# Layer 1's mixer in a 32-graph network: B and C as one product, step sizes beside the gate's product, slice norms spread by one product, two graphs' heads in turn

## The chip, the cores and the metric

One core of a Trainium2 chip runs the whole network in one launch. Times are device microseconds. The time that counts is the median of the runs; a profiled execution shows where it goes. TensorE is called PE below, its weight loads PEld, VectorE DVE, ScalarE ACT, GpSimd POOL and SyncE SP, as the profile has them.

## The reference, cut to what matters

32 graphs of 512 nodes with 256 features pass two layers, each a graph network and a feed-forward part, each on a normed input and added to it. What changes is in the feed-forward part of layer 1, a mixer: every node is softly assigned to 64 slices in each of 8 heads, the slices are averaged into tokens, the 64 tokens of a graph pass a state-space scan in both directions, and the result is handed back to the nodes.

```python
def _L1_ffn_ref(x, ...):
    ...            # sw = softmax over 64 slices, per node and head
    ...            # st = sw-weighted sum of fx / (sum of sw over nodes + 1e-5)
    ot = _hydra(st, ...)
    out = jnp.einsum('bhgc,bhng->bhnc', ot, sw).transpose(0, 2, 1, 3).reshape(B, N, D_INNER)
    return out @ out_w.T + out_b

def _hydra(u, in_w, conv_w, conv_b, dt_bias, A_log, Dp, fcD_w, norm_w, out_w):
    zxbcdt = u @ in_w.T                       # 512 z, 512 x, 64 B, 64 C, 16 dt
    z = zxbcdt[..., :D_INNER]
    xBC = zxbcdt[..., D_INNER:D_INNER + CONV_DIM]
    dt = zxbcdt[..., -2 * H:]
    dt = jnp.concatenate([dt[..., :H], jnp.flip(dt[..., H:], axis=1)], axis=0)
    dt = jax.nn.softplus(dt + dt_bias)
    ...                                       # causal convolution of 3 taps over xBC, then silu
    ...                                       # scan: h = h * exp(-dt * exp(A_log)) + dt * B x; y = C h
    y = y + x_og * jnp.repeat(x_og @ fcD_w.T + Dp, P, axis=-1)
    yg = y * jax.nn.silu(z)
    yg = yg * jax.lax.rsqrt(jnp.mean(jnp.square(yg), -1, keepdims=True) + 1e-05) * norm_w
    return yg @ out_w.T
```

Here D_INNER is 512 (8 heads of 64), and there are 64 tokens for each graph.

## The kernel before

Layer 0 (`layer0_sorted`) fills the first half of the span, with the setup of layer 1 threaded through its end. Layer 1 is `layer1_plain`, a set of Python generators whose steps are laid one after the other at build time; nothing branches on the chip.

Two streams are woven. `attentions()` goes through the 32 graphs one by one: `prepare(b)` loads and norms a graph and makes its masks and projections, `attention(b)` makes the weights (`att`, L1215), the products `avp` (L1248) and `adp` (L1255), and `norm(b)` closes the graph. `mixer(g)` goes through 16 groups of two graphs (GB = 2). The loop at the end of `layer1_plain` draws from `mixer`, and at each of its yields advances `attentions` by the number yielded times PACE. A yield of 7 in `scan` thus stands for some six steps of attention that are written into the queues at this place. After that each engine works off its own queue in order; the order within a queue is nearly that of the code, though the framework's scheduler lets an instruction pass another where it expects it to be ready first.

A group goes through these stages, with the tile names that the profile shows:

- `slices(b, j, yT, rn)`, once for each of the two graphs: norm, logits `lgp`, the softmax `sw` on DVE (L1338 to L1343), the slice sums `yTp`, the transposed weights `swT` whose copy on ACT also accumulates the slice norms, and `rn`, their reciprocal (L1355, L1356). `rn` has one column for each graph and chunk of 128 (two heads by 64 slices) on 128 partitions.
- `tokens`: the products `uTp` (L1367), then `rnp` (L1373), which brings the reciprocals from the partitions to the columns and repeats them over 64 partitions: 16 products of a broadcast column with half of the identity. ACT copies it to `scale`, DVE makes the tokens `uT` (L1380, L1382).
- `scan`, head: `xp` (L1401), the x part of the input projection, transposed; `bcp` (L1410), B and C as two products of 64 rows each; `dtp` (L1429), the step sizes twice in the order of the directions on halves of the partitions, and once more with tokens on partitions (L1394 through `tok_matmul`); `zp` (also L1394), the gate, 512 columns. They are copied or read by `xpad` and `bpad` (ACT), `sp` (DVE L1436, then the softplus) and `z` (ACT Silu, L1451). The convolutions are on DVE (`conv`, L1418 and L1420), their Silu on ACT (L1456, L1463). `la` (L1468) and `seg` (L1482) follow from the step sizes.
- `scan`, middle, after a yield of 7: `gp` (L1488), the products of B and C; `segp` (L1492), from `seg`; `decay` (ACT L1494), `xtp`, `qp`, and `mix` (DVE, to L1511).
- `scan`, after another yield of 7: `yp` (L1518), sixteen products of 64x64 on 64 columns, first the eight heads of graph 0 on partitions 0 to 63, then those of graph 1 on 64 to 127; `y` (DVE L1521 to L1523), the transposes `yTp` (L1528), `oTp` (L1536), `msp` (L1544), which moves the mean squares `ms` to the partitions of the tokens by products with the identity; `rms` (DVE L1547, POOL L1548); then `vp` (L1558) and `v` (ACT L1560).
- `unslice`, for each graph: `outp` (L1568), the sum, and the store.

All PSUM tiles of these stages and of `prepare` come from one tag, "any", with four banks; attention has four of its own ("pv"). The 512-column tiles `scale`, `xT`, `seg`, `decay`, `xk`, `mix`, `back`, `y`, `yT`, `oT` share one tag, "inner", with six buffers. `inT` holds the transposed input projection in the order of the reference: 512 columns of z, 512 of x, 64 of B, 64 of C, 16 of step sizes (DT0 is where those begin, DIN the end). In the profile one fp32 product counts as two passes, each a weight load and a matmul.

Of the kernel before, what the change touches and what calls it, by code (L numbers as in the profile page):

```python
# [8 lines left out]
F32 = mybir.dt.float32  # L9
# [4 lines left out]
AF = mybir.ActivationFunctionType  # L14
# [5 lines left out]
P = 128  # L20
# [846 lines left out]
def layer1_plain(tc, ident, eps, x2s, ranks, adj, w, out, over, ps):  # L867
# [35 lines left out]
    with ExitStack() as ctx:  # L903
# [51 lines left out]
        bc_w = const("bc_w", [S, 2, KW], w["hy_conv_w"][DI:].rearrange("(c p) k -> p c k", p=S))  # L955
        bc_b = const("bc_b", [S, 2], w["hy_conv_b"][DI:].rearrange("(c p) -> p c", p=S))
        skip = const("skip", [P, H], w["hy_D"].partition_broadcast(P))
        dtb = ctile("dtb", [P, 4, H])
        for i in range(4):
            nc.sync.dma_start(dtb[:, i, :], w["hy_dt_bias"].partition_broadcast(P))  # L960
# [18 lines left out]
        for j in range(GB):  # L979
            tri(side[j * G : (j + 1) * G, 0, :], False)  # L980
            tri(side[j * G : (j + 1) * G, 1, :], True)

# [9 lines left out]
        with tc.tile_pool(name="raw", bufs=2, side="right") as raw:  # L992
# [16 lines left out]
            yield from load_T(inT, w["hy_in_w"], "in")  # L1009
# [349 lines left out]
        def tokens(g, yT, rn, uT):  # L1359

            pu, pn = psum("any", f"uTp{g}"), psum("any", f"rnp{g}")
            uv, nv = (p.rearrange("p (k j g) -> p k j g", k=KC, j=GB) for p in (pu, pn))
# [6 lines left out]
            for k in range(KC):  # L1369
                for i in range(P // C):  # L1370
                    half = slice(i * C, (i + 1) * C)
                    for j in range(GB):
                        nc.tensor.matmul(nv[half, k, j, :], rn[:, j, k : k + 1].to_broadcast([P, C]), ident[:, half],  # L1373
                                         start=True, stop=True)
# [9 lines left out]
        def scan(g, uT):  # L1384
# [14 lines left out]
            for k in range(KC):  # L1399
                for c in range(KC):  # L1400
                    nc.tensor.matmul(px[:, k * T : (k + 1) * T], inT[:, c, DI + k * P : DI + (k + 1) * P],  # L1401
                                     uT[:, c, :], start=c == 0, stop=c == KC - 1)
# [3 lines left out]
            pb = psum("any", f"bcp{g}")  # L1406
            for i in range(2):
                c0 = 2 * DI + i * S
                for c in range(KC):
                    nc.tensor.matmul(pb[:S, i * T : (i + 1) * T], inT[:, c, c0 : c0 + S], uT[:, c, :],  # L1410
                                     start=c == 0, stop=c == KC - 1)
# [13 lines left out]
            pd = psum("any", f"dtp{g}")  # L1425
            for j in range(GB):
                for i in range(2):
                    for c in range(KC):
                        nc.tensor.matmul(pd[i * G : (i + 1) * G, j * H : (j + 1) * H],  # L1429
                                         uT[:, c, j * G : (j + 1) * G],  # L1430
                                         inT[:, c, DT0 + i * H : DT0 + (i + 1) * H],
                                         start=c == 0, stop=c == KC - 1)
# [24 lines left out]
            bcT = sb.tile([S, 2, GB, G], F32, tag="bcT", name=f"bcT{g}", bufs=1)  # L1457
# [783 lines left out]
```

## Time and profile before

| | |
|---|---|
| median of 3 runs | 4578.43 us (4575.21 to 4583.15) |
| the profiled execution | 4587.94 us |
| its span, first to last instruction | 4586.1 us |
| mean granted TensorE clock | 0.943 |
| busy: PE, PEld | 4011.0 (87%), 2462.2 (54%) |
| busy: DVE, ACT, POOL | 3391.6 (74%), 2296.8 (50%), 1743.1 (38%) |

Some groups of the profile that belong to the changed code. x counts passes or instructions over the whole run:

| line, tile | shape | count | busy us, mean ns |
|---|---|---|---|
| L1373 rnp, PE | 128x64 weights, 64 columns | 512 | 20.6, 228 |
| L1410 bcp, PE | 128x64 weights, 128 columns | 256 | 31.4, 276 |
| L1429 dtp, PE | 128x64 weights, 8 columns | 512 | 21.8, 204 |
| L1394 dtp, PE | 128x128 weights, 16 columns | 128 | 17.0, 265 |
| L1394 zp, PE | 128x128 weights, 512 columns | 128 | 58.9, 603 |
| L1518 yp, PE | 64x64 weights, 64 columns | 512 | 34.5, 238 |
| L1544 msp, PE | 128x64 weights, 1 column | 128 | 6.4, 202 |
| L1418, L1420 bcT, DVE | 64x128 | 32, 64 | 8.2, 271 and 19.2, 334 |
| L1451 z, ACT | 128x512 | 16 | 9.6, 597 |

Matmuls are pipelined: the printed mean of one pass is its latency, and passes of one row of a timeline overlap. What a row costs PE is read from its start to the start of the next row. A wait is put down to the work that came last before it.

### The profile page before, as it was taken

Reading aid. Unit: us, or ns where it says so; the run is one execution under the profiler, and the core shown is the slowest. Engines: PE = TensorE matmul, PEld = TensorE weight load, DVE = VectorE, ACT = ScalarE, POOL = GpSimd, SP = SyncE. Lnnn points to the kernel's source line nnn. Section 1 sums busy time; section 2 is a strip of 40 time slices with the busy share of each in tenths; the row PEclk is TensorE's granted clock in tenths of the full one; section 3 lists DMA queues with packets and bytes.
Section 4 is the critical chain, followed back from the end, with each engine's and each line's share of the span. In section 5 each row is a group of like instructions: output and inputs, shape, how many; then the busy total and the mean of one; then the engine's idle time right before and its main releaser. Section 6 shows DMA issues by size and latency. Waiting matters only on the chain.

```text
span 4586.1 us, 56206 instructions
## 1 busy us (share of the span) xinstructions
PE 4011.0 (87%) x19287; PEld 2462.2 (54%) x19287; DVE 3391.6 (74%) x7008; ACT 2296.8 (50%) x4756; POOL 1743.1 (38%) x2036
## 2 busy tenths in 40 slices
PE   5567988889988899878997999999999999999987
PEld 4444655556556566445554355555555555555555
DVE  6668888887788877777775777777777777777763
ACT  2344565556655555555664444544544444554432
POOL 2356544654535644353423233222232333322210
PEclk8778999999999999989998999999999999999998
DMA  4447533654436543464422111111111111111100
GB/s 135 155 141 224 179 125 118 203 185 141 142 116 197 182 148 119 121 225 158 140 89 69 35 54 47 56 53 41 47 47 51 54 56 54 53 49 56 40 15 15
DMA packets 235100, 474.09 MB, mean 103 GB/s; under 512 B 38299, under 2 KB 114075, under 8 KB 234804
## 3 DMA queue, kind: packets, MB, share of 16 engines
q0 software_dynamic: 80256, 282.38, 19.2%
q1 hardware_dynamic: 154548, 188.02, 13.2%
q8 instruction: 154, 2.52, 0.2%
q14 instruction: 142, 1.16, 0.1%
HBM read 413.16 MB, written 57.16 MB: 103 GB/s over the span
## 4 chain that ended last, share of the span: by engine, by line
PE 28%; DVE 25%; DMA 7%; POOL 7%; issue 7%; ACT 4%; DVEq 0%; POOLq 0%; SPq 0%; ACTq 0%
DVE att L1215 4%; PE avp L1248 3%; PE clsp L625 3%; PE gatep L625 3%; DVE acc L639 2%; DMA rows<-table,xs 2%; DVE sw L1338 2%; PE po L654 2%; PE yTp L1348 2%; DVE sw L1343 2%; PE adp L1255 2%; DVE sst L1341 2%; PE oTp L1536 1%; PE xp L1401 1%; PE zp L1394 1%
## 5 line engine op out<-in xcount | busy, mean ns | idle before, releaser
L625 PE MATMUL clsp<-xnT,wc 128*128 128x512 f32 x1024 | 535.7, 643 | 83.8 <-ACT cls L627 53.2
L625 PE MATMUL gatep<-xnT,wg 128*128 128x512 f32 x1024 | 505.2, 613 | 13.8 <-ACT gate L627 13.5
L654 PE MATMUL po<-wd,acc 128*128 128x256 f32 x2048 | 458.5, 383 | 10.1 <-DVE h L410 7.2
L1215 DVE SCALAR_TENSOR_TENSOR att<-own,other,mask 128x512 f32<-128x512 f32 x512 | 392.3, 791 | 71.9 <-DMA own<-ownd 71.9
L654 PEld LDWEIGHTS po<-wd,acc 128*128 128x128 f32 x2048 | 391.4, 192 | 78.0 <-issue 11.1
L639 DVE SCALAR_TENSOR_TENSOR acc<-past,fld,acc 128x512 f32<-128x512 f32 x448 | 353.8, 794 | 34.0 <-ACT past L638 25.9
L600 DVE SCALAR_TENSOR_TENSOR best<-rows,xs,best 128x1024 f32<-128x1024 f32 x212 | 275.2, 1302 | 127.2 <-ACT best L594 71.5
L625 PEld LDWEIGHTS gatep<-xnT,wg 128*128 128x128 f32 x1024 | 199.5, 199 | 263.2 <-issue 205.7
L638 ACT ACTIVATE past<-tz,fld 128x512 f32<-128x512 f32 x448 | 291.4, 693 | 78.9 <-DVE acc L639 78.0
L597 POOL DMA_INDIRECT rows<-table,xs x212 | 255.3, 1204 | 166.2 <-DVE best L600 117.1
L625 PEld LDWEIGHTS clsp<-xnT,wc 128*128 128x128 f32 x1024 | 187.6, 203 | 241.0 <-issue 125.1
L634 ACT ACTIVATE acc<-tz,fld 128x512 f32<-128x512 f32 x256 | 198.8, 778 | 229.8 <-PE tz L632 229.4
L1348 PE MATMUL yTp<-sw,x 128*128 128x512 f32 x512 | 262.8, 650 | 57.4 <-DVE sw L1343 54.5
L1248 PE MATMUL avp<-att,hv 128*64 128x512 f32 x1024 | 305.0, 618 | 2.3 <-DVE att L1215 2.3
L436 PE MATMUL pm<-h,adj 128*128 128x258 f32 (+1 forms) x1024 | 180.4, 323 | 111.3 <-DVE keep L441 36.1
L1301 POOL TENSOR_TENSOR mu<-mu,eps 128x16 f32<-128x16 f32 x32 | 113.3, 3540 | 389.8 <-DVE mu L1300 389.7
L627 ACT ACTIVATE cls<-clsp,fld 128x512 f32<-128x512 f32 x256 | 175.7, 686 | 160.2 <-DVE acc L643 76.2
L1336 PE MATMUL lgp<-wsl,x4T 128*128 128x512 f32 x512 | 243.9, 610 | 9.3 <-ACT sw L1337 4.3
L1156 POOL DMA_INDIRECT x<-x2s,ranks x128 | 134.0, 1047 | 293.2 <-DVE att L1215 129.5
L627 ACT ACTIVATE gate<-gatep,fld 128x512 f32<-128x512 f32 x256 | 175.6, 686 | 136.5 <-PE gatep L625 102.1
L555 POOL DMA_INDIRECT xs<-rows_of,order x128 | 154.8, 1209 | 231.9 <-DVE acc L639 99.2
L1568 PE MATMUL outp<-v,swT 128*128 128x256 f32 x1024 | 227.6, 381 | 0.0
(599 smaller groups left out, 8943.0 us busy)
## 6 DMA issues: line engine op xcount, KB each, us to landing
adji<-in_adj SPq DMA_DIRECT2D x128, 256.0 KB
ai<-in_adj SPq DMA_DIRECT2D x128, 256.0 KB
own<-ownd SPq DMA_DIRECT2D x128, 256.0 KB
rows_of<-keep SPq DMA_DIRECT2D x32, 550.0 KB
x<-in_x SPq DMA_DIRECT2D x32, 512.0 KB
x2s<-xs SPq DMA_DIRECT2D x32, 512.0 KB
out<-x SPq DMA_DIRECT2D x32, 512.0 KB
rows<-table,xs POOLq DMA_INDIRECT x212
```

Source lines behind the costliest of these rows:

```text
L597: nc.gpsimd.indirect_dma_start(out=row, out_offset=None, in_=table, in_offset=bass.IndirectOffsetOnAxis(ap=idxs[:, k : k + 1].bitcast(U32) ...
L600: nc.vector.scalar_tensor_tensor(m, row, vals[:, k : k + 1], m, ALU.add, ALU.max)
L625: nc.tensor.matmul(pf, wf[:, c, f * P : (f + 1) * P], xnT[:, c, :], start=c == 0, stop=c == DC - 1)
L627: nc.scalar.activation(o, pf, fn, bias=fld[:, f, bf : bf + 1], scale=1.0 if fn == AF.Gelu else 0.5)
L638: nc.scalar.activation(r, z, AF.Relu, bias=fld[:, f, AT + b : AT + b + 1])
L639: nc.vector.scalar_tensor_tensor(y, r, fld[:, f, CH + b : CH + b + 1], y, ALU.mult, ALU.add)
L654: nc.tensor.matmul(po[:, i, :], acc[f][:, t * P : (t + 1) * P], wd[:, f, :], start=f == 0, stop=f == FC - 1)
L1215: nc.vector.scalar_tensor_tensor(e, own[h], other[:, j, h : h + 1], mask[:, j, :], ALU.max, ALU.mult)
L1248: nc.tensor.matmul(pv[q][k * HO : (k + 1) * HO, :], hv[:, j, h, :HO], weighed[b, h, j], start=j == 0, stop=j == NT - 1)
L1336: nc.tensor.matmul(pf, xnT[:, c, t * P : (t + 1) * P], wsl[:, c, :], start=c == 0, stop=c == DC - 1)
L1348: nc.tensor.matmul(py, xn[:, t, c * P : (c + 1) * P], sw[:, t, :], start=t == 0, stop=t == NT - 1)
L1568: nc.tensor.matmul(po[:, :D], swT[:, k, t * P : (t + 1) * P], v[:, k, :], start=k == 0, stop=k == KC - 1)
```

## The change

The weights' columns in `inT` are put in another order (step sizes, z, x, B, C), so that B and C, and the step sizes and z, lie side by side. B and C become one product with 128 rows out, B on partitions 0 to 63 and C on 64 to 127, one convolution and two Silus. The step sizes are computed once, with tokens on partitions, in one product with the first 256 columns of z, into the bank that also holds B and C; the other 256 columns of z have a bank of their own. The order by direction that `dtp` gave is made by four small DVE sums that read one half of the partitions and write the other. The slice norms are multiplied on DVE with an identity (`spread`, 128x512) and brought to all partitions by one product with a block matrix of ones (`same`). `gp` and `yp` take the two graphs in turn, head by head. `msp` goes; four DVE instructions scale the mean squares and write them to the partitions where `rms` wants them. `same` and `ident2` are filled once by POOL.

```diff
-        bc_w = const("bc_w", [S, 2, KW], w["hy_conv_w"][DI:].rearrange("(c p) k -> p c k", p=S))
-        bc_b = const("bc_b", [S, 2], w["hy_conv_b"][DI:].rearrange("(c p) -> p c", p=S))
+        bc_w = const("bc_w", [P, KW], w["hy_conv_w"][DI:])
+        bc_b = const("bc_b", [P, 1], w["hy_conv_b"][DI:].rearrange("(p o) -> p o", o=1))
-        dtb = ctile("dtb", [P, 4, H])
-        for i in range(4):
+        dtb = ctile("dtb", [P, 2, H])
+        for i in range(2):
+        same = ctile("same", [P, P])
+        nc.gpsimd.memset(same, 0.0)
+        ident2 = ctile("ident2", [P, C])
+        for i in range(P // C):
+            half = slice(i * C, (i + 1) * C)
+            nc.gpsimd.memset(same[half, half], 1.0)
+            nc.gpsimd.tensor_copy(ident2[half], ident[half, half])
-            yield from load_T(inT, w["hy_in_w"], "in")
+            yield from load_T(inT[:, :, 2 * H :], w["hy_in_w"][:DT0], "in")
+            yield from load_T(inT[:, :, : 2 * H], w["hy_in_w"][DT0:], "dt")
...
+            spread = inner(f"spread{g}").rearrange("p (k j g) -> p k j g", k=KC, j=GB)
+            four = [P, KC, GB, G]
+            nc.vector.tensor_tensor(spread, rn.rearrange("p j k -> p k j").unsqueeze(3).to_broadcast(four),
+                                    ident2.unsqueeze(1).unsqueeze(1).to_broadcast(four), ALU.mult)
...
-            for k in range(KC):
-                for i in range(P // C):
-                    half = slice(i * C, (i + 1) * C)
-                    for j in range(GB):
-                        nc.tensor.matmul(nv[half, k, j, :], rn[:, j, k : k + 1].to_broadcast([P, C]), ident[:, half],
-                                         start=True, stop=True)
+            nc.tensor.matmul(pn, same, spread.rearrange("p k j g -> p (k j g)"), start=True, stop=True)
...
-            pb = psum("any", f"bcp{g}")
-            for i in range(2):
-                c0 = 2 * DI + i * S
-                for c in range(KC):
-                    nc.tensor.matmul(pb[:S, i * T : (i + 1) * T], inT[:, c, c0 : c0 + S], uT[:, c, :],
-                                     start=c == 0, stop=c == KC - 1)
-            bpad = sb.tile([S, 2, GB, LP], F32, tag="bpad", name=f"bpad{g}", bufs=1)
-            nc.gpsimd.memset(bpad[:, :, :, : KW - 1], 0.0)
-            nc.scalar.copy(bpad[:, :, :, KW - 1 :],
-                           pb[:S, : 2 * T].rearrange("p (k j l) -> p k j l", k=2, j=GB))
+            pb, pz = psum("any", f"bcp{g}"), psum("any", f"zp{g}")
+            for c in range(KC):
+                nc.tensor.matmul(pb[:, :T], inT[:, c, DIN - P :], uT[:, c, :], start=c == 0, stop=c == KC - 1)
+            first = 2 * H + DI // 2
+            tok_matmul(pb[:, T : T + first], 0, first)
+            tok_matmul(pz[:, : DI // 2], first, DI // 2)
+            bpad = sb.tile([P, GB, LP], F32, tag="bpad", name=f"bpad{g}", bufs=1)
+            nc.gpsimd.memset(bpad[:, :, : KW - 1], 0.0)
+            nc.scalar.copy(bpad[:, :, KW - 1 :], pb[:, :T].rearrange("p (j l) -> p j l", j=GB))
...
-            pd = psum("any", f"dtp{g}")
-            for j in range(GB):
-                for i in range(2):
-                    for c in range(KC):
-                        nc.tensor.matmul(pd[i * G : (i + 1) * G, j * H : (j + 1) * H],
-                                         uT[:, c, j * G : (j + 1) * G],
-                                         inT[:, c, DT0 + i * H : DT0 + (i + 1) * H],
-                                         start=c == 0, stop=c == KC - 1)
-            tok_matmul(pd[:, 2 * H : 4 * H], DT0, 2 * H)
+            pd = pb[:, T : T + 2 * H]
-            nc.vector.tensor_add(v, pd[:, : 4 * H], dtb.rearrange("p i h -> p (i h)"))
+            nc.vector.tensor_add(v[:, 2 * H :], pd, dtb.rearrange("p i h -> p (i h)"))
+            for i in range(2):
+                for j in range(GB):
+                    half = slice(j * G, (j + 1) * G)
+                    nc.vector.tensor_add(v[i * G : (i + 1) * G, j * H : (j + 1) * H],
+                                         pd[half, i * H : (i + 1) * H], dtb[half, 0, :])
...
-            pz = psum("any", f"zp{g}")
-            tok_matmul(pz, 0, DI)
-            nc.scalar.activation(z, pz, AF.Silu)
+            nc.scalar.activation(z[:, : DI // 2], pb[:, T + 2 * H : T + first], AF.Silu)
+            nc.scalar.activation(z[:, DI // 2 :], pz[:, : DI // 2], AF.Silu)
...
-            for i in range(2):
-                conv(bpad[:, i], bc_w[:, i, :], bcT[:, i])
-                dst = bcT[:, 0] if i == 0 else cpad[:, :, 1 : G + 1]
-                nc.scalar.activation(dst, bcT[:, i], AF.Silu, bias=bc_b[:, i : i + 1])
+            conv(bpad, bc_w, bcT)
+            for half, dst in ((slice(0, S), bcT[:S]), (slice(S, P), cpad[:, :, 1 : G + 1])):
+                nc.scalar.activation(dst, bcT[half], AF.Silu, bias=bc_b[half])
...
-            for j in range(GB):
-                half = slice(j * G, (j + 1) * G)
-                for h in range(H):
+            for h in range(H):
+                for j in range(GB):
+                    half = slice(j * G, (j + 1) * G)
                     nc.tensor.matmul(py[half, h * C : (h + 1) * C], heads(mix)[half, h, :],
                                      heads(xk)[half, h, :], start=True, stop=True)
...
-            pm = psum("any", f"msp{g}")
+            rms = sb.tile([P, GB], F32, tag="rms", name=f"rms{g}")
             for j in range(GB):
                 for i in range(P // C):
-                    nc.tensor.matmul(pm[i * G : (i + 1) * G, j : j + 1], ident[:, j * G : (j + 1) * G], ms,
-                                     start=True, stop=True)
-            rms = sb.tile([P, GB], F32, tag="rms", name=f"rms{g}")
-            nc.vector.tensor_scalar(rms, pm[:, :GB], 1.0 / DI, LN_EPS, ALU.mult, ALU.add)
+                    nc.vector.tensor_scalar(rms[i * G : (i + 1) * G, j : j + 1], ms[j * G : (j + 1) * G], 1.0 / DI, LN_EPS,
+                                            ALU.mult, ALU.add)
             nc.gpsimd.tensor_tensor(rms, rms, eps[:, 1:2].to_broadcast([P, GB]), ALU.pow)
```

`xp` reads its columns of `inT` from their new place, and `gp`'s two loops change places like those of `yp`.

More of the change, by code (lines that the diff above doesn't have):

```diff
@@ L1359, in tokens @@
         def tokens(g, yT, rn, uT):
+            spread = inner(f"spread{g}").rearrange("p (k j g) -> p k j g", k=KC, j=GB)
+            four = [P, KC, GB, G]
+            nc.vector.tensor_tensor(spread, rn.rearrange("p j k -> p k j").unsqueeze(3).to_broadcast(four),
+                                    ident2.unsqueeze(1).unsqueeze(1).to_broadcast(four), ALU.mult)
             pu, pn = psum("any", f"uTp{g}"), psum("any", f"rnp{g}")
-            uv, nv = (p.rearrange("p (k j g) -> p k j g", k=KC, j=GB) for p in (pu, pn))
+            uv = pu.rearrange("p (k j g) -> p k j g", k=KC, j=GB)
             for k in range(KC):
@@ L1400, in scan @@
                 for c in range(KC):
-                    nc.tensor.matmul(px[:, k * T : (k + 1) * T], inT[:, c, DI + k * P : DI + (k + 1) * P],
-                                     uT[:, c, :], start=c == 0, stop=c == KC - 1)
+                    x0 = 2 * H + DI + k * P
+                    nc.tensor.matmul(px[:, k * T : (k + 1) * T], inT[:, c, x0 : x0 + P], uT[:, c, :],
+                                     start=c == 0, stop=c == KC - 1)
             xpad = sb.tile([P, KC, GB, LP], F32, tag="xpad", name=f"xpad{g}", bufs=1)
@@ L1456, in scan @@
                 nc.scalar.activation(dst, dst, AF.Silu, bias=conv_b[:, k : k + 1])
-            bcT = sb.tile([S, 2, GB, G], F32, tag="bcT", name=f"bcT{g}", bufs=1)
+            bcT = sb.tile([P, GB, G], F32, tag="bcT", name=f"bcT{g}", bufs=1)
             cpad = sb.tile([S, GB, G + 2], F32, tag="cpad", name=f"cpad{g}", bufs=1)
             nc.gpsimd.memset(cpad[:, :, 0 : G + 2 : G + 1], 0.0)
-            for i in range(2):
-                conv(bpad[:, i], bc_w[:, i, :], bcT[:, i])
-                dst = bcT[:, 0] if i == 0 else cpad[:, :, 1 : G + 1]
-                nc.scalar.activation(dst, bcT[:, i], AF.Silu, bias=bc_b[:, i : i + 1])
+            conv(bpad, bc_w, bcT)
+            for half, dst in ((slice(0, S), bcT[:S]), (slice(S, P), cpad[:, :, 1 : G + 1])):
+                nc.scalar.activation(dst, bcT[half], AF.Silu, bias=bc_b[half])
             la = sb.tile([P, GB, H], F32, tag="la", name=f"la{g}")
@@ L1485, in scan @@
             pg = psum("any", f"gp{g}")
-            for j in range(GB):
-                for i in range(2):
-                    nc.tensor.matmul(pg[j * G : (j + 1) * G, i * G : (i + 1) * G], bcT[:, 0, j, :],
+            for i in range(2):
+                for j in range(GB):
+                    nc.tensor.matmul(pg[j * G : (j + 1) * G, i * G : (i + 1) * G], bcT[:S, j, :],
                                      cpad[:, j, 2 * i : 2 * i + G], start=True, stop=True)
@@ L1514, in scan @@
             py = psum("any", f"yp{g}")
-            for j in range(GB):
-                half = slice(j * G, (j + 1) * G)
-                for h in range(H):
+            for h in range(H):
+                for j in range(GB):
+                    half = slice(j * G, (j + 1) * G)
                     nc.tensor.matmul(py[half, h * C : (h + 1) * C], heads(mix)[half, h, :],
```

## The prediction

> **What bounds the kernel.** I read the page first, then the busy time by stretches of one group, then the chain of waits, then the engines' timelines over one group.
>
> ```profile
> span 4586.1 us, 56206 instructions
> PE 28%; DVE 25%; DMA 7%; POOL 7%; issue 7%; ACT 4%; DVEq 0%; POOLq 0%; SPq 0%; ACTq 0%
> ```
>
> No engine owns the chain: PE and DVE share it. The changed code runs once a group (two graphs, 16 groups), from about 2510 us on. The first xp product of the groups stands at 2637, 2764, 2891 ... 4514: a period near 127 us. One stretch of the busy time:
>
> ```profile
> core 0: us, PE busy (x) PEld busy (x) DVE busy (x) ACT busy (x) POOL busy (x), PEclk, DMA share, GB/s
> 3140.00:3265.00 125.00, 117.61 (x700) 67.63 (x699) 91.24 (x197) 61.56 (x158) 36.84 (x28) 0.99 0.17 52
> ```
>
> PE is busy 94% at full clock, DVE 73%. The chain of waits splits each period:
>
> ```profile
> 3134.01 0.68 DVE sw L1343
> 3134.73 5.40 PE yTp L1348 x8
> ...
> 3182.11 3.84 PE oTp L1536 x32
> 3186.80 1.35 DMA ownd<-turned
> 3188.20 3.36 DMA own<-ownd
> 3191.58 0.75 DVE att L1215
> ```
>
> From 3134.7 to 3186 (tokens and scan) the chain is PE's, row upon row; before and after, it is DVE, POOL and DMA work of attention and slices, where nothing changes. So time saved up to oTp counts; time saved after it does not. The PE rows there, in order of start:
>
> ```profile
> 3144.46 1.15 PE L1373 MATMUL rnp<-ident,rn 128*64 128x64 f32 x32
> 3145.55 0.40 PE L1086 MATMUL maskp<-identb,a 128*128 128x128 bf16 x4
> ...
> 3153.51 1.96 PE L1410 MATMUL bcp<-uT,inT 128*64 128x128 f32 x16
> 3155.31 1.36 PE L1429 MATMUL dtp<-inT,uT 128*64 128x8 f32 x32
> 3156.60 1.07 PE L1394 MATMUL dtp<-inT,uT 128*128 128x16 f32 x8
> 3157.51 3.68 PE L1394 MATMUL zp<-inT,uT 128*128 128x512 f32 x8
> 3161.03 0.83 PE L1086 MATMUL maskp<-identb,a 128*128 128x128 bf16 x12
> ...
> 3176.19 1.90 PE L1518 MATMUL yp<-xk,mix 64*64 64x64 f32 x32
> 3178.01 2.05 PE L1182 MATMUL hp<-wa,x3T 128*128 128x264 f32 x8
> ```
>
> Costs are from start to next start (the printed durations hold the pipe's depth); one fp32 product is two passes.
>
> **The change on PE, per group.**
> Slice norms: 32 passes take 1.09 (3144.46 to 3145.55). New: 2 passes of 512 columns, at zp's 3.52/8 = 0.44: 0.88. Saves 0.21.
> B and C: 16 passes of 64 weight columns take 1.80. New: 8 passes with 128 weight columns and 128 moving ones, as xp's 32 in 3.77 (3149.74 to 3153.51), 0.118 each: 0.94. Saves 0.86.
> Step sizes and gate: 1.29 + 0.91 + 3.52 = 5.72. New: 8 passes of 272 columns and 8 of 256. outp's 256 columns go at 7.02/32 = 0.219, so 8 x 0.233 = 1.86 and 8 x 0.219 = 1.75. Saves 2.11.
> Heads in turn: yp's 32 passes take 1.82, 0.057 each, all of graph 0's half first. rnp, which changes halves every four passes with the same 64 columns, runs at 1.09/32 = 0.034. So 1.09; saves 0.73, 0 if the halves do not overlap. gp's 8 passes (0.39) by the same row 0.27: 0.12.
> Mean-square product: msp's 8 passes (0.33) and minep run while ACT copies oT (3185.99 to 3186.58), and vp waits for that copy, starting at 3186.62. I take 0 for its removal; the copy is the cover, and without it 0.33. The row turned, too, stands behind oT on ACT.
> In all PE loses 4.36 us of work per group.
>
> **What it adds on DVE, and what PE then waits for.**
>
> ```profile
> 3143.86 0.17 DVE L1356 RECIPROCAL rn<-rn 128x4 f32<-128x4 f32 x1
> ...
> 3154.58 1.23 DVE L1304 TENSOR_TENSOR av<-av,mu 128x1024 f32<-128x1024 f32 x1 [2.14 <-POOL mu L1301]
> 3155.72 0.48 DVE L1418 TENSOR_SCALAR xT<-xpad,conv_w 128x128 f32<-128x128 f32 x2
> ...
> 3165.96 1.26 DVE L1482 TENSOR_TENSOR seg<-la,seg_r 128x512 f32<-128x512 f32 x2
> ```
>
> The spread is a 128x512 product like seg's: 0.60 of the queue. It stands between rn and the norm product; rnp began 0.43 after rn, so PE stalls some 0.30 (0.69 with latency, plus 0.05, less 0.43), and all 0.69 in the groups where rn is late already: five of 16 by the timelines. Behind it in DVE's queue stand att, the norm's av rows, uT; uT ends 0.97 before xp starts, so xp is covered, with some 0.4 left.
> v becomes five small sums (about 0.09 of queue each, as la's 3165.54 to 3165.63): +0.36. B and C's convolution falls from six instructions of 64 rows to three of 128 with the same columns (0.20, 0.26, 0.26): -0.72. The rms is four for one, +0.25, in the 3.68 us that DVE idles after y for POOL's hv: free.
> Now the limit. From 3155.72 to seg's end at 3167.22 DVE works without a gap, and PE's segp starts at 3168.90: 1.68 of slack, within 0.1 of that in 13 groups of 16. PE would come 2.97 - 0.09 + 0.12 = 3.0 earlier; seg comes 0.24 later (0.60 of spread, carried over mu, POOL's 3.34 and av; plus 0.36, less 0.72), if the queue's order stays. So the gain at segp is 1.68 - 0.24 = 1.44 at least, and 3.0 at most, if the order changes so that the step-size work goes first: masks, att and x rows stand between it now, and its input is ready 0.94 + 1.86 = 2.8 after xp's end, against 4.0. That an order can change is seen on ACT, where xT's first Silu (L1456) runs ahead of the exponential (L1438) that the code names first. I take 1.5, next to the lower row, since DVE's stretch is the nearest evidence and has no gap.
> [...]
> [...]
> ACT: the gate as two halves of 256 costs 2 x 0.40 for 0.60 (+0.2; ht's 128x256 copy is 0.39), B and C's copy less 0.1. gp has 3.0 of slack behind cpad.
> POOL's and SP's queues: five more small fills and copies and two DMAs fewer, once, in the first layer's time: 0. The weights' loads keep their ten steps.
>
> **Sum.** Per covered group: 1.5 at segp, 0.73 at yp (mix was ready 1.2 before yp, so PE sets it), less 0.13 for late norms (0.39 in 5 of 15): 2.1. Fifteen groups: 31.5. The last group has no cover: +0.5 (spread), -0.5 (seg, at best), -1.0 (yp takes 3.3 there at a low clock): -1. Total -32.5. The profiled execution (4587.9; 1.8 of it outside the span) would be 4555; the runs' median is 9.5 lower, so **4546**. Bounds of the terms: segp 1.44 to 3.0, yp 0 to 0.8, late norms 0 to 0.69, so 0.7 to 3.8 a group: 4567 to 4520.
>
> **Rivals.**
> *PE's whole saving lands* (0.12). If PE's total is the bound, 4.36 x 16 = 70: 4508. For: PE 94% busy. Against: some 76 of the 127 us of the chain are DVE, POOL and DMA.
> *Absorbed* (0.10). The spread falls behind one of the norm's 1.2 us rows in DVE's queue, PE stalls 1.9 more at the norm product and uT's slack of 0.97 is gone; yp does not speed up. 1.44 - 1.2 = 0.24 a group: about 4575. For: rnp waited for a norm row in five groups. Against: rn itself is past those rows by then in ten.
> *Slower: the shared bank is held* (0.20). Before, the step sizes' bank was free once v was read; now it stays until the first gate half is through ACT. z runs at 3163.77 to 3164.37 in the trace. After zp PE turns three masks, each in a bank of the same four; two will be held by the gate. If the third mask (3161.5 now, so about 3158.6) waits for z's present place, PE stands 5.7, reaches segp 2.7 later than before, and keeps 0.73 at yp: +2.0 x 15 = +30, 4608. It turns to a loss once the half ends after about 3162.3 (3158.6 + 3.0 + 0.73). For: ACT reloads its table six times a group at 1.28 each, which delays the gate. Against: the first half's product is ready about 3156.4, when ACT waits, and the silu table is loaded next anyway.
> *Forecast* (0.58): 4520 to 4567.
>
> A measurement of this kernel tells some 0.2% (9 us) from no change. Faster by more: 0.58 + 0.12 + a third of the absorbed case = 0.73; within: 0.07; slower: 0.20. The range reaches down to the full PE saving, 4508, and up to 4594, half-way into the slower case.
>
> **What would show it.** Right: bcp 8 passes near 0.95; 272 and 256 columns in 3.6 together; yp near 1.1; segp waiting for seg by 1 us or so; period down by 2. Wrong: yp still 1.8, PE idle at the third mask after the gate, or over 1 us at the norm product; more table loads than the 96 of now.

## The result, and the profile after

The changed kernel takes 4595.4 us (median of 8 runs, 4591.5 to 4604.1) against 4578.0 for the kernel before (8 runs, 4564.0 to 4583.2): ratio 1.0045, 95% interval [1.0031, 1.0058]. It is 0.45% slower; 4546 was forecast. The profiled execution has a span of 4597.5 us. Its page, span and chain:

```profile
span 4597.5 us, 53823 instructions
...
DVE 30%; PE 19%; POOL 8%; DMA 8%; issue 7%; ACT 6%; DVEq 0%; POOLq 0%; SPq 0%; ACTq 0%
```

2383 instructions are gone, and of the chain PE has 19% where it had 28%, DVE 30% for 25%. The same stretch of 125 us in the busy time by stretches (columns PE, PEld, DVE, ACT, POOL, then the granted clock):

```profile
3140.00:3265.00 125.00, 112.50 (x570) 63.71 (x568) 88.71 (x189) 58.07 (x150) 39.02 (x28) 0.96 0.16 51
```

PE was busy 117.61 of 125 and is 112.50: the work was taken off PE, and PE waits longer. PE's rows at the head of one group, in order of start:

```profile
3648.28 1.97 PE L1380 MATMUL uTp<-yT,wfxT 128*64 128x128 f32 x32
3650.03 1.08 PE L1257 MATMUL avp<-att,hv 128*64 128x512 f32 x4
3651.04 1.04 PE L1264 MATMUL adp<-att,hv 128*32 128x512 f32 x2
3652.01 1.13 PE L1382 MATMUL rnp<-spread,same 128*128 128x512 f32 x2
...
3657.14 1.93 PE L1257 MATMUL avp<-att,hv 128*64 128x512 f32 x6
...
3662.68 1.06 PE L1417 MATMUL bcp<-uT,inT 128*128 128x128 f32 x8
3663.57 2.00 PE L1402 MATMUL bcp<-inT,uT 128*128 128x272 f32 x8
3665.41 1.89 PE L1402 MATMUL zp<-inT,uT 128*128 128x256 f32 x8
...
3675.70 0.45 PE L1491 MATMUL gp<-cpad,bcT 64*64 64x64 f32 x8 [1.80 <-ACT cpad L1466]
```

By starts, B and C take 0.89, the 272 columns 1.84, the 256 columns 1.72 and the norm product 0.96: each within 0.1 of its forecast. But six passes of attention (`avp`, `adp`) now stand between `uTp` and `rnp`, and `gp` waits for `cpad`, C after its convolution and Silu. The waits of PE from 2640 to 4420 us (in total, times, longest):

```profile
PE yTp L1357 <- DVE sw L1352: 52.3, 36, 2.4
PE gp L1491 <- ACT cpad L1466: 35.3, 14, 4.0
PE yp L1521 <- DVE mix L1514: 13.5, 8, 2.3
```

Before, `gp` did not wait in any of 14 groups, and `yp` waited 4.8 us in all. Where the time went is read best if a group is cut at three rows: from the start of `yp` to the end of `rn` (slices of the next group), from there to the first `xp` product (tokens), and from there to `yp` (scan). Means over 13 groups, worked out from the starts and ends in the timelines, for this kernel and for the experiments that follow:

| run | yp to rn | rn to xp | xp to yp |
|---|---|---|---|
| before | 94.49 | 6.21 | 26.33 |
| after | 93.05 | 9.07 | 26.21 |
| e2, own banks | 93.86 | 9.03 | 25.61 |
| e3, no spread | 93.04 | 6.04 | 27.90 |
| e4, heads only | 94.69 | 5.92 | 26.32 |
| e8, no spread, own banks | 94.72 | 5.92 | 24.11 |
| e9, bias in four | 92.86 | 9.22 | 24.85 |
| e10, neither, bias in four | 93.40 | 6.21 | 24.17 |
| e11, no spread, bias in four | 92.51 | 6.12 | 26.35 |
| e12, own banks, bias in four | 93.20 | 9.19 | 24.01 |
| e13, spread in halves | 93.56 | 7.72 | 25.55 |
| e14, idle spread | 93.14 | 5.73 | 24.82 |
| e15, filled wait | 93.07 | 9.12 | 25.61 |

After against before: 1.44 gained, 2.86 lost, 0.12 gained: 1.3 us a group slower, 20 us over fifteen groups, which is nearly all of the difference (0.45% of 4578 is 20.6). So two questions: why do the tokens take 2.86 longer, and why does the scan, from which PE lost most work, not get shorter?

### The profile page after: what moved, and what is told of

Same layout as the page of the kernel before. It is cut to its first block, busy times and chain, and to the rows that moved or that the text cites. A ratio compares the mean times of both kernels' runs of the same rounds, so it can differ in the third digit from the quotient of the medians.

```text
span 4597.5 us, 53823 instructions
## 1 busy us (share of the span) xinstructions
PE 3976.0 (86%) x18039; PEld 2429.3 (53%) x18039; DVE 3406.4 (74%) x7088; ACT 2298.8 (50%) x4772; POOL 1748.2 (38%) x2041
## 3 DMA queue, kind: packets, MB, share of 16 engines
q8 instruction: 144, 2.36, 0.2%
## 4 chain that ended last, share of the span: by engine, by line
DVE 30%; PE 19%; POOL 8%; DMA 8%; issue 7%; ACT 6%; DVEq 0%; POOLq 0%; SPq 0%; ACTq 0%
DVE att L1224 5%; PE clsp L625 3%; PE gatep L625 3%; DVE acc L639 2%; DMA rows<-table,xs 2%; DVE sw L1347 2%; DVE sw L1352 2%; DVE sst L1350 2%; PE yTp L1357 2%; PE po L654 2%; PE oTp L1539 1%; POOL mu L1310 1%; POOL x L1165 1%; PE hp L1191 1%; DMA xs<-rows_of,order 1%
## 5 line engine op out<-in xcount | busy, mean ns | idle before, releaser
L436 PEld LDWEIGHTS pm<-h,adj 128*128 128x128 f32 x1024 | 151.7, 214 | 143.9 <-issue 78.2
```

The lines of the kernel that those rows point to most:

```text
L436: nc.tensor.matmul(pm[:, : c1 - c0], a[:, i, t * P : (t + 1) * P], h[:, i, c0:c1], start=i + c0 == 0, stop=i + 1 == NT and c0 > 0)
```

## The experiments

All ratios are to the kernel before, timed beside each experiment on the same chip, with 95% intervals.

### One part at a time

Two suspects. Theory A, the shared bank: B and C, the step sizes and half the gate sit in one bank, so the step sizes start late. Theory B, the spread: PE does attention's products ahead of `rnp` and `xp`, and they are then missing ahead of `gp`.

**e1**, the sums ahead of ACT's copy of B and C:

```diff
-            nc.scalar.copy(bpad[:, :, KW - 1 :], pb[:, :T].rearrange("p (j l) -> p j l", j=GB))
...
+            nc.scalar.copy(bpad[:, :, KW - 1 :], pb[:, :T].rearrange("p (j l) -> p j l", j=GB))
             nc.vector.scalar_tensor_tensor(e, v, -1.0, v, ALU.mult, ALU.min)
```

> The changed kernel, with ACT's copy of B and C written behind the five step-size sums, so that the sums do not wait for a copy out of the same bank. Theory A (the shared bank puts the step sizes late, C's Silu later still, and PE idles at gp for some 2.5 us a group): the exponential starts 1 to 2 us earlier after xp than the 11.5 of the changed kernel, cpad ends near 15.5 after xp instead of 16.7 to 17.5, the wait of gp for cpad falls from about 30 us over 12 groups to under 5, and the time falls by 15 to 35 us, to 4560 to 4580. Theory B (the spread on DVE takes the cover: it lengthens the way to xp, and what attention work PE does there is missing before gp): gp still waits, now for cpad or seg, and the time stays within 8 us of 4595.

Measured: 4600.2, ratio 1.006 [1.0041, 1.0079]. The exponential of the step sizes did start earlier, at 10.0 us after the first `xp` product where the changed kernel has 11.7, as theory A expected, but the time did not fall. This was tried with the spread in place only, and so, as with e2, the square further down shows that it does not clear the shared bank.

**e2**, a bank of their own for the step sizes and the first gate half:

```diff
-            pb, pz = psum("any", f"bcp{g}"), psum("any", f"zp{g}")
+            pb, pd, pz = (psum("any", f"{n}p{g}") for n in ("bc", "dt", "z"))
...
-            tok_matmul(pb[:, T : T + first], 0, first)
+            tok_matmul(pd[:, :first], 0, first)
...
-            pd = pb[:, T : T + 2 * H]
+            pz0, pd = pd[:, 2 * H : first], pd[:, : 2 * H]
```

> The changed kernel with B and C in one bank and the step sizes with the first gate half in another. Theory A: as the run before, the copy and the sums no longer wait for each other; gp's wait under 10 us over 12 groups, time 4560 to 4580. Theory B: within 8 us of 4595. If the bank of four that it takes more is what counts, PE waits at the third mask and the time is above 4595.

Measured: 4593.2, ratio 1.0044 [1.0028, 1.0061]; no difference. Alone this speaks against theory A; below it turns out that the cost was hidden by the spread's.

**e3**, the norms by 16 small products, as before the change:

```diff
-            nc.tensor.matmul(pn, same, spread.rearrange("p k j g -> p (k j g)"), start=True, stop=True)
+            for k in range(KC):
+                for i in range(P // C):
+                    half = slice(i * C, (i + 1) * C)
+                    for j in range(GB):
+                        nc.tensor.matmul(nv[half, k, j, :], rn[:, j, k : k + 1].to_broadcast([P, C]), ident[:, half],
+                                         start=True, stop=True)
```

> The changed kernel with the 16 small products for the slice norms as before. Theory B: rnp follows uTp at once, PE has as much attention work before gp as in the kernel before, so gp's wait falls below 15 us over 12 groups and the time falls by 15 to 25, to 4570 to 4580. Theory A: the step sizes are as late as before, gp waits as long, and the time stays within 8 us of 4595.

Measured: 4579.2, ratio 1.0012 [0.9999, 1.0025]: 15 us better than the changed kernel, and rn to xp is back at 6.04. But xp to yp rose by 1.7. The timeline of e3, DVE and POOL, at `mix`:

```profile
3166.74 0.68 DVE L1514 TENSOR_TENSOR mix<-mix,back 128x512 f32<-128x512 f32 x1
3166.99 2.64 POOL L1338 TENSOR_TENSOR x<-x,outb 128x1024 f32<-128x1024 f32 x1 [5.56 <-ACT x L1144]
3167.46 2.73 DVE L1515 TENSOR_TENSOR mix<-mix,decay 128x512 f32<-128x512 f32 x1
```

POOL adds the output bias to the rows of a coming graph, work that nobody waits for. The DVE instruction that starts while it runs takes 2.73 us in place of 0.69. This meeting was there in 14 of e3's groups:

```profile
L1515 DVE TENSOR_TENSOR mix<-mix,decay x14: 2716/2720/2832, 2655.8 to 4306.6; 128x512 f32<-128x512 f32 x14
```

(minimum, median and maximum in ns). The changed kernel has it in 5 groups, e2 in 9, the kernel before in 1. It is not what made xp to yp longer in e3, though: without it the same step, e9 to e11 in the table above, still adds 1.5 us, since 42 passes of attention in place of 26 stand between `xp` and `gp` in most groups.

**e4**, the kernel before with only the two graphs' heads in turn (`gp`, `yp`):

```diff
-            for j in range(GB):
-                half = slice(j * G, (j + 1) * G)
-                for h in range(H):
+            for h in range(H):
+                for j in range(GB):
+                    half = slice(j * G, (j + 1) * G)
```

> The kernel before with nothing changed but the order of the products of yp and gp (graphs in turn). Both theories: yp falls from 1.82 to 1.1 us in a covered group, mix is ready 1.2 us before yp now, so 0.7 a group comes off the path: 4567 plus or minus 5. If what the path saves there is given back to DVE or ACT behind it, 4578.

Measured: 4576.3, ratio 1.0005 [0.9994, 1.0017]. `yp` is 0.7 us shorter, and nothing comes of it; 4567 was expected if the saving counted. After `yp`, first in the kernel before:

```profile
3177.46 2.36 POOL L1329 TENSOR_TENSOR x<-x,outb 128x1024 f32<-128x1024 f32 x1 [5.82 <-ACT x L1135]
3178.85 1.52 DVE L1523 TENSOR_TENSOR y<-y,z 128x512 f32<-128x512 f32 x1
```

and in e4:

```profile
3155.80 0.69 DVE L1522 TENSOR_TENSOR y<-y,yp 128x512 f32<-128x512 f32 x1 [2.42 <-PE yp L1518]
3155.87 2.36 POOL L1329 TENSOR_TENSOR x<-x,outb 128x1024 f32<-128x1024 f32 x1 [5.83 <-ACT x L1135]
3156.52 2.25 DVE L1523 TENSOR_TENSOR y<-y,z 128x512 f32<-128x512 f32 x1
```

POOL's addition begins as `y` does, and `y` times `z` ends only after it (3158.77 against 3158.23). In the kernel before this row had 1.52 us, and its end lies just as far behind POOL's (3180.37 against 3179.82). What `yp` gains, `y` waits: in most groups of both kernels the transposes start 4.3 us after `yp` does.

### POOL's addition

Theory C: a DVE instruction with two SBUF inputs can't end while POOL's addition runs; its rival, D, is that the saving on `yp` is lost for another reason. e5 and e6 leave out the bias `out_b` of the mixer's output; e7 and e8 are complete.

```diff
-            nc.gpsimd.tensor_add(xt, xt, outb.unsqueeze(1).to_broadcast([P, NT, D]))
```

> The kernel before without POOL's add of the output bias to the graph's rows (x4's L1329, 128x1024, 2.4 us); the bias is left out of the output. Theory C (DVE's two-input fp32 products from SBUF cannot end while POOL works on a two-input one, so y*z ends with POOL's add and not with yp): y*z falls from 1.52 to 0.69 us, yTp and oTp come 0.8 earlier after xp (31.5 instead of 32.4), and the time falls by 8 to 14. Theory D (yp's saving is lost for another reason, the queue behind it): y*z stays at 1.52 and the time within 5 us of the kernel before.

**e6** is e5 with the heads in turn.

> The same with the heads in turn. Theory C: with POOL's add gone the 0.7 us of yp reaches oTp, which stands 30.8 after xp, 0.7 before its place in the run without the turn; the time is 7 to 12 below that run. Theory D: as little difference between the two as between the kernel before and the one with the turn alone, under 4 us.

**e7** has the heads in turn, and the addition in four:

```diff
-            nc.gpsimd.tensor_add(xt, xt, outb.unsqueeze(1).to_broadcast([P, NT, D]))
+            for t in range(NT):
+                nc.gpsimd.tensor_add(xt[:, t, :], xt[:, t, :], outb)
```

> Heads in turn, and POOL's bias add in four adds of 128x256 (0.6 us each); nothing is left out. Theory C: DVE gets in between two of them, y*z takes at most 1.3 and mostly 0.7 us, oTp comes 1 us or more earlier, time 15 to 25 below the kernel before (4550 to 4560). Theory D: no change from the heads alone, 4575.

**e8** is the changed kernel with the edits of e2 and e3 together.

> The changed kernel with both suspects undone: the small products for the slice norms as before, and the step sizes with the first gate half in a bank of their own. If the spread costs the 15 us that its undoing showed and the shared bank the rest, xp to yp takes some 25.4 (as with own banks alone), uTp to xp 8.1 as before, and the time is 10 to 20 below the kernel before. If the saving on PE in the scan is idle time whatever the order (the scan is a chain of latencies on ACT and DVE), it stays within 6 us of the kernel before.

| run | median us | ratio to before |
|---|---|---|
| e5, no bias | 4548.6 | 0.9953 [0.9938, 0.9968] |
| e6, heads in turn, no bias | 4532.9 | 0.9913 [0.9898, 0.9928] |
| e7, heads in turn, bias in four | 4547.6 | 0.9942 [0.9929, 0.9955] |
| e8, no spread, own banks | 4528.9 | 0.9912 [0.9897, 0.9928] |

Without the addition the heads in turn are worth 16 us (e6 against e5), about 1 us a group; with it in one piece, nothing. Four small additions bring 29 of the 42 us that leaving them out brings with the heads in turn (e7 and e6, against e4): in e7 `y` times `z` takes 0.69 in every group, and `mix` 1.21 at most. Theory C stands for an instruction that starts while the addition runs (in the profiles of before and after all 20 of them end 0.55 us behind it), and it had the effect too small: it expected 8 to 14 us for e5 and 7 to 12 from e5 to e6, where 22 and 16 came. And e8 shows that e2 and e3 do not add up to what they bring together: 61 us below the changed kernel by the ratios, where the one brought nothing and the other 15.

### The square, without the meeting

So spread and shared bank were tried in all four combinations, each with the addition in four.

> The changed kernel with one edit: POOL's addition of outb to the group's rows as four adds of 128x256 in place of one of 128x1024 (complete). It and the three runs beside it form a square, spread or not by shared bank or not, all without the long meeting of DVE and POOL. Theory E (the spread costs by the place that attention's work takes ahead of it, 1.5 us or more of each group, and the shared bank costs by late sums and a late exponential, about 1 us or more a group, whether or not DVE meets POOL at the mask rows): this one is the slowest of the four, 4560 to 4580, 45 us or more above the one with neither; the before of this call near 4573. Rival F (both cost only through the meeting: they move mix or y onto POOL's add): all four lie within 12 us of each other, near 4505 to 4520. In both, no mix row over 1.6 us.

> The changed kernel with the step sizes and the first gate half in a bank of their own, the norms spread by 16 small products as before, and POOL's addition as four adds (complete). Both theories: y rows fall from 2.13 to near 1 us and the heads in turn keep their 0.7, so 4500 to 4516, some 1.3 to 1.6% below before. It is the candidate for the fastest; if it stays at the 4529 that it had with one long add, the long add did not matter here.

> The changed kernel with the norms spread by 16 small products as before and POOL's addition as four adds (complete); only the shared bank is left of the two suspects. Theory E: 4520 to 4540, 15 to 30 above the one with neither, with the exponential near 11.4 us after the first xp product against near 9; rival F: within 12 of it. The 4579 of the same kernel with one long add had 14 of 16 mix rows at 2.7 us; without those at least 28 us must go.

> The changed kernel with the step sizes and the first gate half in a bank of their own and POOL's addition as four adds (complete); only the spread is left of the two suspects. Theory E: 4545 to 4570, 35 or more above the one with neither, with uT's product to the next xp product some 2.5 us longer in each group; rival F: within 12 of it.

| median us, ratio | with the spread | 16 small products |
|---|---|---|
| shared bank | e9 4574.2, 1.0006 [0.9993, 1.002] | e11 4546.6, 0.9939 [0.9918, 0.9959] |
| own banks | e12 4558.1, 0.9965 [0.9952, 0.9978] | e10 4515.9, 0.9875 [0.9854, 0.9895] |

Theory E stands: the spread costs 42 us with own banks and 28 with the shared one, the shared bank 16 and 31, both 58. Rival F, all within 12 us, falls. (E had expected 15 to 30 for the bank in e11; 31 came.) e10 is the fastest version, 1.25% below the kernel before: it keeps the joined products, the heads in turn and the mean squares without a product, has the addition in four, and is without the spread and the shared bank.

*The spread.* The table of sections has it in rn to xp: 9.0 to 9.2 in every kernel with the whole spread, 5.7 to 6.2 without. The same stretch of PE in e10, to be held against the rows shown of the changed kernel:

```profile
3599.81 1.97 PE L1377 MATMUL uTp<-yT,wfxT 128*64 128x128 f32 x32
3601.56 1.15 PE L1383 MATMUL rnp<-ident,rn 128*64 128x64 f32 x32
...
3604.98 1.93 PE L1257 MATMUL avp<-att,hv 128*64 128x512 f32 x6
3606.84 3.84 PE L1412 MATMUL xp<-uT,inT 128*128 128x128 f32 x32
```

and what DVE does for it in the changed kernel:

```profile
3649.41 0.17 DVE L1365 RECIPROCAL rn<-rn 128x4 f32<-128x4 f32 x1
3649.50 0.15 DVE L1303 TENSOR_SCALAR mu<-mu 128x16 f32<-128x16 f32 x1
3649.55 0.75 DVE L1224 SCALAR_TENSOR_TENSOR att<-own,other,mask 128x512 f32<-128x512 f32 x1
3650.22 0.68 DVE L1372 TENSOR_TENSOR spread<-rn,ident 128x512 f32<-128x512 f32 x1
...
3656.17 0.68 DVE L1390 TENSOR_TENSOR uT<-uT,bfx 128x512 f32<-128x512 f32 x1
```

The reciprocal ends at 3649.58 and the spread at 3650.90, since an attention row stands between; `rnp` starts at 3652.01, behind six attention passes that the scheduler put ahead of it; `uT` ends at 3656.85, and `xp` starts 2.15 later, behind more of them. On average `rnp` starts 2.00 after the reciprocal's end, and `uT` ends 1.83 ahead of `xp` (before 1.10). Before, `rnp` started 0.4 after the reciprocal in ten of 14 groups and up to 2.2 ahead of it in the rest, as its first columns need graph 0 alone: 0.23 ahead on average. Between `uTp` and `xp` PE has 34 attention passes in nearly every group, where it had 18 in most and 20 on average. They are then missing ahead of `gp`: between `xp` and `gp` there are 26, against 32 before and 42 in e10.

*The shared bank.* Times after the first `xp` product, means over 14 groups. The exponential of the step sizes begins at 11.6 in e9 and 12.3 in e11, at 9.7 in e12 and 10.2 in e10, and before the change at 9.2. ACT's rows of the changed kernel:

```profile
3665.61 0.27 ACT L1423 COPY bpad<-bcp 128x128 f32<-128x128 f32 x1
...
3668.15 0.38 ACT L1454 ACTIVATE z<-bcp 128x256 f32<-128x256 f32 x1 [0.43 <-DVE sp L1440]
...
3669.16 1.28 ACT L1443 ACT_TABLE_LOAD   x1
3670.45 0.23 ACT L1443 ACTIVATE sp<-sp 128x32 f32<-128x32 f32 x1
```

The copy of B and C starts at 3665.61, 0.04 us after PE's product of 272 columns has ended in the same bank (3663.57 and 2.00), although B and C themselves were done 1.8 us before. In none of the 14 groups does it start before that product's end. With a bank of its own it starts behind its own product; the same rows in e12, 4.77 after `xp` in place of 6.61:

```profile
3647.84 1.06 PE L1418 MATMUL bcp<-uT,inT 128*128 128x128 f32 x8
3648.93 0.27 ACT L1424 COPY bpad<-bcp 128x128 f32<-128x128 f32 x1 [0.30 <-PE bcp L1418]
```

Behind the late copy DVE's sums are late too, 8.5 after `xp` in e9 against 7.2 in e12 (and 7.3 in e1, which has them ahead of the copy), and the exponential is behind them on ACT, at 11.45 after `xp` here, and `cpad` behind it. The gate's first half waits for DVE's sums although its product was ready early, but so it does in e12 and e10, where it still shares a bank with the step sizes. By what way a shared bank holds the copy back no run shows.

### What the spread's 42 us are made of

**e13** writes the spread in halves, one for each graph, on the kernel of e12; **e14** puts the spread's instruction on the kernel of e10, with its result not used.

```diff
-            nc.vector.tensor_tensor(spread, rn.rearrange("p j k -> p k j").unsqueeze(3).to_broadcast(four),
-                                    ident2.unsqueeze(1).unsqueeze(1).to_broadcast(four), ALU.mult)
+            for j in range(GB):
+                nc.vector.tensor_tensor(spread[:, :, j, :], rn[:, j, :].unsqueeze(2).to_broadcast([P, KC, G]),
+                                        ident2.unsqueeze(1).to_broadcast([P, KC, G]), ALU.mult)
```

> The changed kernel with own banks and POOL's addition as four adds, and the spread written by two DVE instructions, one for each graph's 256 columns, in place of one (complete). By PE's queue this puts 26 passes of avp and adp between uTp and the next xp product in a group, against 34 with one instruction and 20 with the 16 small products. Theory H (the spread costs by the order: attention products that stand ahead of rnp and xp and are then missing as cover ahead of gp): the cost falls with the passes, to some 6/14 of 42 us: 4530 to 4540, and gp's wait for cpad falls from 25 us in the window to near 12. Rival G (it costs by DVE's time between rn and rnp): two instructions take longer than one, so 4558 or more.

> The kernel with neither suspect and POOL's addition as four adds, with the spread's DVE instruction put back ahead of uTp, but its result not used: the norms still go by 16 small products (complete). PE's queue has 19 passes of avp and adp between uTp and the next xp product, as without the spread. Theory H: the instruction's 0.69 us on DVE alone costs at most that, 0 to 11 us over the 4515.9 without: 4513 to 4527. Rival G: most of the 42 us, 4545 to 4558.

Measured: e13 4561.5, ratio 0.9976 [0.9963, 0.999]; e14 4528.5, ratio 0.9902 [0.9889, 0.9916]. The instruction alone costs 13 us of the 42, a little over theory H's 11 and far from rival G's 29 or more. But H's own number falls too: in e13 rn to xp went down by 1.5 us, xp to yp went up by as much, and the time did not move, so that it lies where G had it (4558 or more) and not at H's 4530 to 4540. The passes that no longer stand ahead of `xp` stand ahead of `gp`, and `gp`'s wait fell as H said, from 25.3 us in 14 groups to 11.6. So the other 29 us go with `rnp` hanging on the spread, and putting attention's passes back does not recover them. By what way they come about no run takes apart.

**e15** and **e16** test the clock. The busy time by stretches, changed kernel, around a `gp` (its wait ends at 3419.76 and lasts 3.96 us):

```profile
3410.00:3414.00 4.00, 4.00 (x27) 1.45 (x27) 3.90 (x15) 2.74 (x8) 0.12 (x1) 1.00 0.00 0
3414.00:3418.00 4.00, 1.79 (x12) 0.16 (x8) 2.60 (x15) 3.92 (x6) 1.31 (x3) 1.00 0.00 0
3418.00:3422.00 4.00, 2.24 (x12) 0.80 (x12) 2.20 (x7) 3.95 (x7) 0.21 (x2) 0.67 0.02 4
3422.00:3426.00 4.00, 4.00 (x22) 3.51 (x20) 0.78 (x3) 2.77 (x5) 2.23 (x1) 0.50 0.27 66
```

After the wait the granted clock is 0.50. Theory K: this low clock is what the wait costs. Its rival L: the clock costs nothing, or the filling delays `gp`. e15 fills the wait, in the changed kernel, with products whose result nothing reads; e16 does the same in e9:

```diff
             pg = psum("any", f"gp{g}")
+            for i in range(3):
+                nc.tensor.matmul(pg[:, 2 * G :], ident[:S], bcT[:S].unsqueeze(1).to_broadcast([S, 3, GB, G]), start=True, stop=True)
```

> The changed kernel with three products of no use (64x128 weights, 384 columns, six passes, about 2 us of PE a group) right ahead of gp in PE's queue, written to columns of gp's bank that nothing reads (complete otherwise). PE waits there anyway for cpad, 1.8 to 4.0 us a group. Theory K (the wait lets the granted clock fall, and the slow products behind it, segp, then decay and mix, cost the time): the clock in the 12 us after gp rises from a mean near 0.79 to 0.95 or more, segp to yp falls from 8.65 to near 7.5, and the kernel is 10 to 25 us faster than the changed one, 4570 to 4585, although PE does 32 us more work. Rival L (the low clock goes along with the wait but costs nothing, or the products delay gp): 4592 to 4615.

> e9 (the changed kernel with POOL's addition as four adds) with the same six passes of no use ahead of gp. There the clock fell in 5 groups of 14, those with a wait of 2.9 us or more. Theory K: those groups alone gain, the mean clock in the groups rises from 0.976 to 0.985 or so, and the kernel is 3 to 12 us faster than e9's 4574: 4560 to 4572. Rival L: 4572 to 4590.

Measured: e15 4582.6, ratio 1.0025 [1.0012, 1.0037]; e16 4577.2, ratio 1.0003 [0.9986, 1.0021]. The clock did what theory K said: its mean over the 12 us after `gp` rose from 0.78 to 0.95 in e15, and from 0.89 to 1.00 in e16. The time followed only in part: e15 gains 0.2% on the changed kernel, some 9 us, though the two intervals overlap; e16 gains nothing, as rival L had it. `segp` to `yp` stayed (8.65, then 8.63), against K's 7.5; but half of `segp` now runs ahead of `gp`, and xp to yp, which that does not touch, fell by 0.6. For the same reason the filling is no clean test: from `gp`'s end to `mix` it is 2.9 us in e15 where it was 4.3, but `gp` itself starts 18.2 us after `xp` where it started at 17.0, and most of the gain is used up. So giving the clock back by such filling brings little; what the low clock alone costs stays open.

For e12 against e10 the sum does not close. A group is 2.6 us longer. `gp` waits 25.3 us in 14 groups against 3.4, 1.6 us a group, but other waits shrink, and PE's idle time as a whole grows by 0.9 a group (13 groups, 10.1 against 9.2). The clock's mean over the groups is 0.980 against 0.984, some 0.5 of 126 us. Open stays the rest, and how far another order of the queues could hide the spread.

## Why the prediction was wrong

*Sizes on PE: right.* B and C 0.89 (0.94 forecast), the two token products 3.56 (3.61), the norm product 0.96 (0.88), `yp` 1.12 (1.09). The work went from PE, and no time with it: PE is busy 1637 us from 2640 to 4420 where it was 1680.

*The step that failed first: "uT ends 0.97 before xp starts, so xp is covered, with some 0.4 left", and with it the stall of "some 0.30" at the norm product.* I priced the spread as 0.6 us inserted in DVE's queue, with every other queue unchanged: 0.13 a group. Measured: rn to xp is 2.86 longer: 2.23 more ahead of `rnp`, 0.73 more behind `uT`, and 0.10 less between them. PE stalls little at `rnp` itself (3.3 us in all); the scheduler put attention products there. What I named as cover was moved by the very wait that it was to cover. The rival "Absorbed" came nearest: it had a late norm product and the cover gone, but as a stall of PE, at 1.2 us a group, and a saving beside it.

*The second: "I take 1.5" at segp, and "gp has 3.0 of slack behind cpad".* The number came: `segp` starts 17.52 us after `xp` where it started at 18.98, 1.46 earlier. That is luck, for it came by another wait. PE did not stand at `segp` for `seg`, as the prediction has it (one such wait in 14 groups, 0.67 us), but at `gp` for `cpad`, 2.5 us a group. The two rows before the change:

```profile
3165.14 0.39 ACT L1463 ACTIVATE cpad<-bcT,bc_b 64x128 f32<-64x128 f32 x1
3168.51 0.46 PE L1488 MATMUL gp<-cpad,bcT 64*64 64x64 f32 x8
```

and `cpad` in the changed kernel, 0.05 ahead of the `gp` shown above:

```profile
3675.25 0.40 ACT L1466 ACTIVATE cpad<-bcT,bc_b 64x128 f32<-64x128 f32 x1
```

The slack of 3.0 is just what PE was to gain by its 3.0 us of saved work, so nothing was left of it, and `cpad` came 1.0 later besides (16.95 after `xp` on average, before 15.92). Nor did the gain pass on. The changed kernel's DVE timeline behind `gp`:

```profile
3676.48 0.28 DVE L1509 TENSOR_TENSOR gm<-gp,side 128x128 f32<-128x128 f32 x1
3679.11 0.17 DVE L1507 TENSOR_TENSOR dq<-qp,skip 128x8 f32<-128x8 f32 x1 [2.34 <-PE qp L1505]
3679.19 0.68 DVE L1512 TENSOR_TENSOR mix<-gm,sp 128x512 f32<-128x512 f32 x1
...
3681.72 2.72 DVE L1514 TENSOR_TENSOR mix<-mix,decay 128x512 f32<-128x512 f32 x1
```

`mix` stands behind `dq`, and `dq` waits for `qp`, the third product behind `gp` on PE. On average `gp` ends 17.52 us after `xp` (before 19.05) and `mix` starts at 21.83 (before 22.05): of 1.53, 0.22 is left, as those products take longer after a long wait of `gp` (4.3 us from `gp` to `mix` on average; 3.04 in five groups at a clock of 1.00, 5.54 in four at 0.50; 3.1 in e10, all at 1.00). The prediction had no term for a lower clock in these groups. Then `mix` meets POOL's addition, here as in five groups. I followed the gain to `segp` and not to the row that it feeds. That it was there to be had is shown by e8 and e10: xp to yp is 2.2 us shorter with own banks and no spread.

*The shared bank: not in the sum.* The 1.5 at `segp` has no term for it: I left out that ACT's copy of B and C waits for the whole product of 272 columns beside it (it starts behind that product's end in all 14 groups). The exponential is about 2 us later by the bank, and the bank costs 16 us with the spread and 31 without (e9 to e12).

*Heads in turn, 0.73 a group: right with a condition I did not see.* Alone they gave nothing (e4), as POOL's addition set the end of `y` times `z`; without it, 1 us a group (e6 against e5). In the changed kernel POOL meets `mix`, not `y`, and the stretch from `yp` to its transposes is 0.87 shorter.

*The mean-square product, at 0: right.* `vp` waits for the copy of `oT` in its place, 0.6 us in each of 14 groups. *The slower rival, a mask that waits for the gate's bank:* no mask waits for the gate in the changed kernel (in e10 eight do, 5.0 us in all); slower was right, this mechanism not: that its 4608 lies near the measured 4595 is luck.

Added up: tokens 2.86 against 0.13, scan 0.12 gained against 1.5, the rest 1.44 gained against 0.73: 3.4 us a group, 51 us over fifteen groups, of the 53 between the forecast's -32.5 and the +20.6 that the ratio gives.

## What to carry to other kernels

An instruction put between two engines can cost more than its own length, by what the scheduler does around the new wait (here 13 us alone, 42 with a product hanging on it); read the queue order on both sides of it before calling anything covered. Follow a gain through to the row that the next stage waits for, and look there for an idle engine's work in the way: here a bias addition on POOL, cut in four, gave 0.6% (e7 against e4), more than the change took. Two faults can hide each other, so an edit that changes nothing alone should be tried again with the other one undone: e2 and e3 brought 0 and 15 us, together 61.

## What the runs showed of the hardware

- DVE and POOL: a 128x512 instruction of DVE with two fp32 inputs in SBUF takes 0.69 us. One that starts while POOL's 128x1024 addition is running ends 0.55 us behind the addition, in all 15 cases before and all 5 in the changed kernel, and so takes up to 2.72 us there and 2.83 in e3 (1.52 in most groups before and 2.25 in e4, where less of the addition was left). The nine that start 0.19 to 0.36 us ahead of the addition keep their 0.69, and so does `y` plus `yp`, one input of which is in PSUM, in 13 cases in the midst of it. With additions of 128x256 (e7) `mix` and `y` take at most 1.21. POOL's own addition took 2.64 in e3 and 2.36 in e4. By what way the two engines hold each other up no run shows.
- The clock after a wait of PE: in the changed kernel four waits of `gp` of 3.1 to 4.0 us and three of 2.36 us were each followed by a granted clock of 0.50, for 6.8 to 10.0 us, and one of 2.94 by the same for 3.4 us; PE had no other wait over 0.1 us in the 14 us ahead of them. After the six of 1.7 to 1.8 us it stayed at 1.00 for 9 us or more, and in five of these groups it fell later, behind `yp`'s own wait of 2.3 us for the `mix` that met POOL's addition. In e12 ten waits of 2.1 to 2.3 us were followed by a fall in six groups and by none in four.
